# Layer 0 of a four-layer convolution chain: five of nine depthwise taps computed by VectorE and GpSimd, Gelu over pairs of PSUM banks, stores of two steps sent together

## The chip, the cores and the metric

The kernel runs on one core of a Trainium2 chip, all in float32 but for one quantised convolution in a later layer. The time is the device time of that core in microseconds, the median of several runs. A profiled execution gives one more time, its own, and the trace from which all views are taken. In the views PE is TensorE (PEld its weight loads), DVE is VectorE, ACT is ScalarE, POOL is GpSimd and SP is SyncE; SPq is the queue of DMA issues on SP.

## The reference, cut to what matters

The input x has the shape (4, 16, 512, 512): four images, 16 channels. Four layers follow one another. The change concerns layer 0 only, a block with window attention:

```python
pos = depthwise_conv3x3(x, pos_w)          # one 3x3 filter for each channel, padding 1
x = x + pos + pos_b
win = windows_8x8(x * alpha1 + beta1)      # 64 tokens in a window, 16 channels
q, k, v = win @ qkv_w.T + qkv_b            # 2 heads of 8 channels, q scaled by 8 ** -0.5
out = softmax(q @ k.T) @ v
x = x + (out @ proj_w.T + proj_b)
h = gelu((x * alpha2 + beta2) @ fc1_w.T + fc1_b)    # 16 -> 64
x = x + h @ fc2_w.T + fc2_b                # 64 -> 16
```

Layers 1 to 3 are a quantised 3x3 convolution with a batch norm over the whole tensor, a residual pair of 3x3 convolutions, and a 3x3 convolution with a small MLP. Layer 1 needs the largest absolute value of all that layer 0 gives, so it begins after the last store of layer 0.

## The kernel before, in words

`window_attention` works in 64 steps (`STEPS`). A step holds 16 units, by u and vv from 0 to 3. A unit is 32 partitions (two blocks of 16 channels) by 8 rows of 64 columns: 8 windows of 64 tokens, the 512 columns of a matmul. The order of the instructions on every engine is the order in which they are written (`manual_schedule`): nothing is reordered, and an engine whose next instruction waits holds all that is written behind it on that engine. The SP queue, which issues nearly all DMAs, is one of them.

A step n works on three steps' data at once:

- **Attention of step n**, a loop over k = 0 to 7 (half a block column each). `scores` (L353) writes four banks, ScalarE's Exp (L361) takes them in two pairs to e; `values` (L338) turns the values into yt; `attend` (L374) gives two banks, which `divide` transposes on VectorE (L389), takes the reciprocal of the sums (L394) and multiplies on GpSimd (L396); `turn_back` (L403) transposes the result into o, one or more k later. In the loop stand also `turn_keys` (L310: DMAs that bring the next step's y into the order of keys), `send` (L90: up to 5 stores a k) and `highest_output` (L452: one maximum of a finished output).
- **The MLP of step n**: `project` (L409, and L414 on VectorE, which adds to y), then 16 `hidden` units (L421), each with a Gelu on ScalarE (L426) from one bank. `output` (L432, and L437 on VectorE, into xo) of step n stands in step n + 1, after its first scores. xo is one buffer that two steps fill; after an odd step its 32 stores are listed, and `send` issues them later.
- **Queries of step n + 1** (`query`, L319; the copies to g are L324 on ScalarE and L326 on VectorE) and the **depthwise convolution of step n + 2** (L287), both woven into the MLP by a string of letters: d is one tap for one u (four matmuls of 32x32 with 512 columns), q one query, h one hidden unit. When all 9 taps for 4 u are done, `position` adds the bias and writes y (L302 on VectorE for two u, L298 on ScalarE for two). `highest` (L329) takes the maximum of the next y.

The depthwise convolution multiplies the shifted input (x with a border of one) by a 32x32 diagonal matrix of the tap's weights (`taps`, which is `small`, an identity, times `tap0`); nine taps add up in PSUM. A float32 matmul stands in the trace as two records. PSUM has eight banks: 0 to 3 as two pairs, 4 to 7 single. x has two buffers, y three, e three, hid sixteen (one bank each).

After the last step the output of u = 0 to 2 is placed between the last hidden units, with its stores on two queues, SP and GpSimd.

## Time and profile before

| what | value |
|---|---|
| median of 3 runs | 5842.46 us (5837.79 to 5846.63) |
| the profiled execution, its own time | 5832.97 us |
| its span | 5831.2 us |
| TensorE busy | 5512.4 us (95%) |
| VectorE busy | 3723.4 us (64%) |
| ScalarE busy | 3464.1 us (59%) |
| GpSimd busy | 707.4 us (12%) |
| mean granted TensorE clock | 0.987 |
| DMA | 677.47 MB, mean 116 GB/s |

Layer 0 takes the first 21 or so of 40 equal slices of the span. A line of the costliest groups reads: line, engine, operation, output<-input, shape, count | busy us, mean ns of one | idle time of the engine before them, and what ended it. A line of the timeline reads: start, duration, engine, line, operation, count, and in brackets the idle time before it and its releaser. A row of the windows view gives for one stretch its length, the busy time of PE, PEld, DVE, ACT and POOL with counts, the granted clock of TensorE (1.00 is full), the DMA share and GB/s. Matmul records overlap[...], so busy TensorE time is not the sum of their durations.

### The profile page before, as it was taken

The page shows a single profiled execution, that of the slowest core. Times are in us where ns is not written, and L with a number is a line of the kernel's source. Part 1 is how long each engine was busy: PE and PEld are TensorE (multiplying, and loading weights), DVE is VectorE, ACT ScalarE, POOL GpSimd, SP SyncE. Part 2 cuts the span into 40 slices and gives each one's busy share as a digit, 9 for nine tenths or more (in the row PEclk, how much of TensorE's full clock was granted, in tenths as well). Part 3 has the DMA queues.
Part 4 walks back from the last instruction along what each step waited for, and adds up shares of the span by engine and source line. Part 5 has one row for each costly group of instructions (what it writes and reads, how often), then busy time and mean ns, then how long its engine had stood idle before and what let it go on. Part 6 is the DMA issues. An engine that isn't in the chain of part 4 may idle for free. (4 is left out here: it accounts for less than half of the span.)

```text
span 5831.2 us, 268523 instructions
## 1 busy us (share of the span) xinstructions
PE 5512.4 (95%) x120912; PEld 3058.4 (52%) x120912; DVE 3723.4 (64%) x5806; ACT 3464.1 (59%) x4739; POOL 707.4 (12%) x692
## 2 busy tenths in 40 slices
PE   7999999999999999999999676999999999999999
PEld 5666666666666666666666333333333333333333
DVE  4666666666666666666666564666666666666666
ACT  4777777777777777777776453444444444444444
POOL 1111111111111111111111451000000000000000
PEclk9999999999999999999999898999999999999999
DMA  2232323233333333332332796666666666666663
GB/s 78 69 77 68 81 67 72 69 79 70 78 72 75 75 72 77 71 79 69 79 70 47 170 252 169 168 169 171 165 171 167 169 171 166 170 167 170 171 165 103
DMA packets 626194, 677.47 MB, mean 116 GB/s; under 512 B 355856, under 2 KB 485008, under 8 KB 616848
## 3 DMA queue, kind: packets, MB, share of 16 engines
q1 hardware_dynamic: 624240, 658.76, 47.3%
q8 instruction: 953, 15.61, 1.1%
q14 instruction: 201, 1.65, 0.1%
q0 software_dynamic: 512, 1.05, 0.1%
q10 hardware_dynamic: 288, 0.39, 0.0%
HBM read 222.45 MB, written 134.48 MB: 61 GB/s over the span
## 5 line engine op out<-in xcount | busy, mean ns | idle before, releaser
L361 ACT ACTIVATE e<-pair 128x1024 f32<-128x1024 f32 x1024 | 992.9, 1022 | 436.7 <-PE pair L353 436.0
L287 PE MATMUL pair<-x,taps 32*32 32x512 f32 x18432 | 1082.2, 600 | 2.2 <-DVE y L302 1.2
L1205 ACT ACTIVATE hid<-tb,vec 128x512 f32<-128x512 f32 x1024 | 620.0, 688 | 518.1 <-PE tb L1197 518.0
L389 DVE STREAM_TRANSPOSE a<-bank 128x512 f32<-128x512 f32 x1024 | 669.8, 692 | 346.5 <-PE bank L374 313.3
L396 POOL TENSOR_TENSOR t<-a,r 128x512 f32<-128x512 f32 x512 | 542.0, 1059 | 2662.2 <-DVE r L394 2598.5
L426 ACT ACTIVATE hid<-bank,f1b 128x512 f32<-128x512 f32 x1024 | 648.3, 687 | 345.2 <-PE bank L421 281.6
L353 PE MATMUL pair<-g,y 32*128 32x128 f32 x16384 | 762.8, 288 | 29.5 <-ACT y L298 25.8
L353 PEld LDWEIGHTS pair<-g,y 32*128 32x128 f32 x16384 | 650.4, 187 | 189.6 <-issue 77.4
L421 PE MATMUL bank<-y,fc_e 32*32 32x512 f32 x8192 | 738.3, 606 | 1.0 <-DVE y L414 1.0
L1207 DVE TENSOR_SCALAR hid<-tb,vec 128x512 f32<-128x512 f32 x1024 | 695.7, 742 | 2.7 <-PE tb L1197 2.6
L1197 PE MATMUL tb<-ye,mat 32*128 32x512 f32 x4096 | 637.7, 624 | 0.3 <-DVE hid L1207 0.3
L374 PE MATMUL bank<-e,yt 64*32 64x128 f32 x32768 | 610.0, 276 | 28.3 <-DVE yt L346 21.4
L287 PEld LDWEIGHTS pair<-x,taps 32*32 32x32 f32 x18432 | 495.4, 103 | 171.2 <-issue 66.3
L374 PEld LDWEIGHTS bank<-e,yt 64*32 64x32 f32 x32768 | 465.6, 106 | 127.3 <-issue 99.1
L1217 PE MATMUL tb<-hid,mat 128*32 128x512 f32 x4096 | 466.0, 595 | 41.6 <-DVE hid L1207 41.6
L1197 PEld LDWEIGHTS tb<-ye,mat 32*128 32x128 f32 x4096 | 267.0, 183 | 323.4 <-issue 219.9
L1122 PE MATMUL tb<-zo,cw 64*32 64x512 f32 x3096 | 362.8, 594 | 14.8 <-issue 8.9
L338 PE MATMUL bank<-mat,y 128*128 128x128 f32 x2048 | 338.9, 288 | 36.1 <-DVE xo L437 36.0
L1122 PE MATMUL tb<-xo,cw 64*32 64x512 f32 x3096 | 365.0, 599 | 8.4 <-issue 6.6
L1122 PE MATMUL tb<-xe,cw 64*32 64x512 f32 x3072 | 360.3, 599 | 0.0
L1122 PE MATMUL tb<-ho,cw 64*32 64x512 f32 x3072 | 355.2, 591 | 3.1 <-issue 3.1
L1122 PE MATMUL tb<-ze,cw 64*32 64x512 f32 x3072 | 356.8, 594 | 0.0
(180 smaller groups left out, 7051.7 us busy)
## 6 DMA issues: line engine op xcount, KB each, us to landing
x<-in_xw_dram SPq DMA_DIRECT2D x64, 1320.0 KB
zo<-ze SPq DMA_DIRECT2D x512, 128.5 KB
ho<-he SPq DMA_DIRECT2D x512, 128.5 KB
xo<-xe SPq DMA_DIRECT2D x512, 128.5 KB
y<-y SPq DMA_DIRECT2D x2048, 32.0 KB
tx<-x SPq DMA_DIRECT2D x256, 256.0 KB
out_dram<-xe SPq DMA_DIRECT2D x128, 512.0 KB
x<-xo SPq DMA_DIRECT2D x1008, 64.0 KB
```

What stands on the lines that cost most here:

```text
L287: nc.tensor.matmul(bank(u)[quad(vv)], taps[quad(u), tap, :], xts[n][quad(u), vv, dy : dy + WS, dx : dx + BW], start=tap == 0, stop=tap == 8,)
L353: nc.tensor.matmul(bank(u)[:, P * jj : P * jj + P], y2[quad(u), vv, jl + jj].rearrange("p w t -> p (w t)"), g[quad(u), vv, jl + jj].rearra ...
L361: nc.scalar.activation(e[:, 2 * i : 2 * i + 2].rearrange("p u j t -> p u (j t)"), pairs[i], AF.Exp,)
L374: nc.tensor.matmul(bank(4 + 2 * (k % 2) + w)[quad(u), P * jj : P * jj + P], t[half, U * jj + u, w : w + 2].rearrange("p d c -> p (d c)"), ...
L389: nc.vector.transpose(a[:, 512 * w : 512 * w + 512], bank(4 + 2 * (k % 2) + w))
L396: engine.tensor_tensor(t.rearrange("p b w c -> p w b c"), top, r.unsqueeze(3).to_broadcast([P, 2, 16, C]), ALU.mult,)
L421: nc.tensor.matmul(b[quad(k)], fc1[quad(vv), quad(k)], y[quad(vv), u, :], start=True, stop=True,)
L426: nc.scalar.activation(hd, b, AF.Gelu, bias=f1b)
L1122: nc.tensor.matmul(p[r][_quad(2 * f + w)], weights[_half(r), odd, dx, :], src[_half(r), f, dx : dx + W], start=dx == 0, stop=dx == 2,)
L1197: nc.tensor.matmul(p[q], w1[_quad(q), 1 - par, :], inner(src)[_quad(q), f, :], start=True, stop=True,)
L1205: nc.scalar.activation(hd, p[q], AF.Relu, bias=v("l3_b1"))
L1207: nc.vector.tensor_scalar(hd, p[q], v("l3_b1"), 0.0, ALU.add, ALU.max)
```

## The change

Taps 4 to 8 are no longer matmuls. VectorE multiplies tap 8 into a buffer `rest` and adds tap 7 (`begin_rest`: 4 tensor_scalar, 4 scalar_tensor_tensor); GpSimd adds taps 4, 5 and 6 (`add_rest`: twelve times a tensor_scalar into one buffer `rt` and a tensor_tensor that adds it to `rest`). TensorE keeps taps 0 to 3 and adds `rest` by a fifth matmul with `small`. Of the twelve pieces for step n + 3 seven are written at the end of step n behind `begin_rest`, and five in the next step's loop over k, each after a `divide`. The two first steps keep nine taps.

All of PSUM becomes four pairs. Gelu takes a pair of banks, 1024 elements, at a time; `divide` transposes a pair at once; all four positions are on VectorE. The woven string of the MLP becomes ten d, eight h, two q, eight h. e has two buffers, hid eight of a pair each. The 32 stores of two steps are sent at k = 1, ahead of that k's `turn_keys`, where there were five at every k. The last step's output is no longer woven in.

```diff
@@ -169,11 +169,13 @@
     wts = ctx.enter_context(tc.tile_pool(name="w0w", bufs=1))
     ps = ctx.enter_context(tc.tile_pool(name="w0p", bufs=1, space=PSUM))
 
-    pairs = [ps.tile([P, 2, 512], F32, name=f"pair{i}") for i in range(2)]
-    singles = [ps.tile([P, 512], F32, name=f"bank{i}") for i in range(4)]
+    pairs = [ps.tile([P, 2, 512], F32, name=f"pair{i}") for i in range(4)]
 
     def bank(i):
-        return pairs[i // 2][:, i % 2, :] if i < 4 else singles[i - 4]
+        return pairs[i // 2][:, i % 2, :]
+
+    def base(k):
+        return 4 + 2 * ((k + 1) % 2)
 
     def quad(i):
         return slice(32 * i, 32 * i + 32)
@@ -270,6 +272,7 @@
     g = pa.tile([P, V, NJ, NH, T], F32, name="g")
     o = pa.tile([P, V, NJ, NH, T], F32, name="o")
     most = pa.tile([P, STEPS], F32, name="most")
+    rest = pa.tile([P, V, WS, BW], F32, name="rest")
     yts = [pa.tile([P, 4 * U, 3, C], F32, name=f"yt{i}") for i in range(3)]
     for t in yts:
         nc.gpsimd.memset(t, 1.0)
@@ -280,28 +283,48 @@
     def by_row(ap):
         return ap.rearrange("p (a j x) -> p a j x", a=WS, x=WS)
 
-    def depthwise(n, tap, u):
-
+    def shifted(n, tap, rows, vv):
         dy, dx = divmod(tap, 3)
+        return xts[n][rows, vv, dy : dy + WS, dx : dx + BW]
+
+    def depthwise(n, tap, u, n_taps=5):
+
         for vv in range(V):
+            if tap < 4 or n_taps == 9:
+                w, src = taps[quad(u), tap, :], shifted(n, tap, quad(u), vv)
+            else:
+                w, src = small[quad(u)], rest[quad(u), vv]
             nc.tensor.matmul(
-                bank(u)[quad(vv)], taps[quad(u), tap, :],
-                xts[n][quad(u), vv, dy : dy + WS, dx : dx + BW],
-                start=tap == 0, stop=tap == 8,
-            )
+                bank(u)[quad(vv)], w, src, start=tap == 0, stop=tap == n_taps - 1
+            )
+
+    def begin_rest(n):
+        every = slice(0, P)
+        for vv in range(V):
+            nc.vector.tensor_scalar(
+                rest[:, vv], shifted(n, 8, every, vv), tap0[:, 8:9], None, ALU.mult
+            )
+        for vv in range(V):
+            nc.vector.scalar_tensor_tensor(
+                rest[:, vv], shifted(n, 7, every, vv), tap0[:, 7:8], rest[:, vv],
+                ALU.mult, ALU.add,
+            )
+
+    def add_rest(n, i):
+        at, vv = divmod(i, V)
+        t = px.tile([P, WS, BW], F32, tag="rt", name=f"rt{n}_{i}", bufs=1)
+        nc.gpsimd.tensor_scalar(
+            t, shifted(n, 4 + at, slice(0, P), vv), tap0[:, 4 + at : 5 + at], None, ALU.mult
+        )
+        nc.gpsimd.tensor_tensor(rest[:, vv], rest[:, vv], t, ALU.add)
 
     def position(n):
 
         y = px.tile([P, U, N], F32, tag="y", name=f"y{n}", bufs=3)
         for u in range(U):
-            if u // 2:
-                nc.scalar.activation(
-                    by_window(y[:, u]), by_row(bank(u)), AF.Identity, bias=v("pos_b")
-                )
-            else:
-                nc.vector.tensor_scalar(
-                    by_window(y[:, u]), by_row(bank(u)), v("pos_b"), None, ALU.add
-                )
+            nc.vector.tensor_scalar(
+                by_window(y[:, u]), by_row(bank(u)), v("pos_b"), None, ALU.add
+            )
         return y
 
     def turn_keys(y, vv):
@@ -333,7 +356,7 @@
     def values(k):
 
         vv, jl = k // 2, 4 * (k % 2)
-        b, t = bank(4 + 2 * (k % 2)), yts[k % 3]
+        b, t = bank(base(k)), yts[k % 3]
         for jj in range(4):
             nc.tensor.transpose(
                 b[:, P * jj : P * jj + P],
@@ -356,7 +379,7 @@
                     g[quad(u), vv, jl + jj].rearrange("p h t -> p (h t)"),
                     start=True, stop=True,
                 )
-        e = px.tile([P, U, 4, P], F32, tag="e", name=f"e{n}_{k}", bufs=3)
+        e = px.tile([P, U, 4, P], F32, tag="e", name=f"e{n}_{k}", bufs=2)
         for i in range(2):
             nc.scalar.activation(
                 e[:, 2 * i : 2 * i + 2].rearrange("p u j t -> p u (j t)"),
@@ -372,7 +395,7 @@
                 for w in range(2):
                     half = slice(64 * w, 64 * w + 64)
                     nc.tensor.matmul(
-                        bank(4 + 2 * (k % 2) + w)[quad(u), P * jj : P * jj + P],
+                        bank(base(k) + w)[quad(u), P * jj : P * jj + P],
                         t[half, U * jj + u, w : w + 2].rearrange("p d c -> p (d c)"),
                         e[half, u, jj, :],
                         start=True, stop=True,
@@ -385,8 +408,9 @@
     def divide(k, n, engine):
 
         a = px.tile([P, 1024 + 2 * C], F32, tag="a", name=f"a{n}_{k}")
-        for w in range(2):
-            nc.vector.transpose(a[:, 512 * w : 512 * w + 512], bank(4 + 2 * (k % 2) + w))
+        nc.vector.transpose(
+            a[:, 0:1024], pairs[base(k) // 2].rearrange("p w n -> p (w n)")
+        )
         top = a.rearrange("p (w n) -> p w n", w=2)[:, :, 0:512]
         top = top.rearrange("p w (b c) -> p w b c", c=32)[:, :, :, 0:C]
         low = a[:, C : 1024 - C].rearrange("p (w n) -> p w n", w=2)[:, :, 0 : 512 - C : 32]
@@ -407,24 +431,29 @@
             for u in range(U):
                 for vv in range(V):
                     nc.tensor.matmul(
-                        bank(4 + (u + 2) % 4)[quad(vv)], wo[h][quad(u)], o[quad(u), vv, :, h, :],
+                        bank(4 + u)[quad(vv)], wo[h][quad(u)], o[quad(u), vv, :, h, :],
                         start=h == 0, stop=h == 1,
                     )
         for u in range(U):
             nc.vector.scalar_tensor_tensor(
-                y[:, u], bank(4 + (u + 2) % 4), pb, y[:, u], ALU.add, ALU.add
-            )
-
-    def hidden(y, u, vv, b, n):
+                y[:, u], bank(4 + u), pb, y[:, u], ALU.add, ALU.add
+            )
+
+    def hidden(y, u, vv, b):
 
         for k in range(4):
             nc.tensor.matmul(
                 b[quad(k)], fc1[quad(vv), quad(k)], y[quad(vv), u, :],
                 start=True, stop=True,
             )
-        hd = px.tile([P, N], F32, tag="hid", name=f"hid{n}_{u}_{vv}", bufs=16)
-        nc.scalar.activation(hd, b, AF.Gelu, bias=f1b)
-        return vv, hd
+
+    def gelu(pair, name):
+        hd = px.tile([P, 2, N], F32, tag="hid", name=name, bufs=8)
+        nc.scalar.activation(
+            hd.rearrange("p w n -> p (w n)"), pair.rearrange("p w n -> p (w n)"),
+            AF.Gelu, bias=f1b,
+        )
+        return hd
 
     def output(y, xo, hids, us, banks, n):
 
@@ -495,7 +524,7 @@
     for n in range(2):
         for tap in range(9):
             for u in range(U):
-                depthwise(n, tap, u)
+                depthwise(n, tap, u, 9)
         xts[n + 2] = load(n + 2)
         ys[n] = position(n)
     highest(0)
@@ -504,6 +533,9 @@
     for h in range(NH):
         for vv in range(V):
             query(ys[0], h, vv, bank(vv))
+    begin_rest(2)
+    for i in range(7):
+        add_rest(2, i)
     last, xo = None, None
     nc.scalar.preload_act_table_set("natural_log_exp_and_others")
     for n in range(STEPS):
@@ -518,7 +550,7 @@
             elif what == "d" and ahead:
                 depthwise(n + 2, taken[at], at)
                 taken[at] += 1
-                if taken == [9] * U:
+                if taken == [5] * U:
                     ys[n + 2] = position(n + 2)
 
         values(0)
@@ -533,16 +565,19 @@
             ts[k - 1] = divide(k - 1, n, nc.gpsimd)
             if 1 < k < 7:
                 turn_back(ts[k - 2], k - 2)
+            if k == 1:
+                send(8 * U)
             if k % 2 and more:
                 turn_keys(ys[n + 1], k // 2)
+            if k < 6 and ahead:
+                add_rest(n + 2, k + 6)
             highest_output()
-            send(5)
         nc.scalar.preload_act_table_set("gelu_and_others")
         attend(es[7], 7)
         ts[7] = divide(7, n, nc.gpsimd)
         for k in (5, 6, 7):
             turn_back(ts[k], k)
-        free = iter((4, 5, 6, 7, 4, 5))
+        free = iter((6, 7, 4, 5, 6, 7))
         for i, what in enumerate("qqddddqqqqdddddd"):
             block(what, i, bank(next(free)) if what == "q" else None, True)
         if more:
@@ -557,24 +592,29 @@
 
 
 
-        hids, units = [], itertools.cycle((6, 7, 4, 5))
-        for i, what in enumerate("ddddhdhddhqhddhqhddhdhddhdhddhdhddhdhddddhdh"):
+        hids, units = [], iter((2, 3, 2, 0, 3, 2, 3, 2))
+        for i, what in enumerate(10 * "d" + 8 * "h" + "qq" + 8 * "h"):
             if what == "h":
-                q = len(hids)
-                hids.append(hidden(y, q // 4, i % 4, bank(next(units)), n))
-                if not more and q in (5, 9, 13):
-                    u = q // 4 - 1
-                    output(y, xo, hids[q - 5 : q - 1], (u,), (u,), n)
-                    send(8, queues)
+                u, at = len(hids) // 4, i % 4
+                if at % 2 == 0:
+                    pair = pairs[next(units)]
+                hidden(y, u, at, pair[:, at % 2])
+                if at % 2:
+                    hd = gelu(pair, f"hid{n}_{u}_{at}")
+                    hids += [(at - 1, hd[:, 0]), (at, hd[:, 1])]
             else:
-                block(what, i, bank(next(units)) if what == "q" else None)
+                block(what, i, bank(i % 4) if what == "q" else None)
+        if n + 3 < STEPS:
+            begin_rest(n + 3)
+            for i in range(7):
+                add_rest(n + 3, i)
         if n + 4 < STEPS:
             xts[n + 4] = load(n + 4)
         if more:
             nc.scalar.preload_act_table_set("natural_log_exp_and_others")
-        last = (y, xo, hids, range(U), (5, 4, 6, 7), n)
-    output(y, xo, hids[12:], (3,), (3,), n)
-    send(8, queues)
+        last = (y, xo, hids, range(U), (7, 5, 6, 4), n)
+    output(*last)
+    send(8 * U, queues)
     highest_output(2 * U)
     return nc.values_load(flag[0:1, 0:1], min_val=0, max_val=1)
```

## The prediction, made before the change was run

> **What bounds the kernel now.** I first read the page's busy times by engine, then its costliest groups, then engine times by stretch for one step of layer 0 (64 steps, about 3,115 of the 5,831 us), then the timelines of ScalarE, VectorE and GpSimd in it. The maximum over y (L329) runs once a step; from 54.25 to 3171.18 us it starts 63 times more, so a step lasts 3116.9 / 63 = 49.5 us. Let t0 be the end of a step's last turn-back (L403); one t0 is 1395.4, the next 1444.6.
>
> ```profile
> L287 PE MATMUL pair<-x,taps 32*32 32x512 f32 x18432 | 1082.2, 600 | 2.2 <-DVE y L302 1.2
> L396 POOL TENSOR_TENSOR t<-a,r 128x512 f32<-128x512 f32 x512 | 542.0, 1059 | 2662.2 <-DVE r L394 2598.5
> L426 ACT ACTIVATE hid<-bank,f1b 128x512 f32<-128x512 f32 x1024 | 648.3, 687 | 345.2 <-PE bank L421 281.6
> ```
>
> The largest TensorE group is the depthwise (18432 records, 288 a step), and GpSimd has one operation of 1059 ns for each of eight k, with 2662 us idle. The step has three stretches:
>
> ```profile
> core 0: us, PE busy (x) PEld busy (x) DVE busy (x) ACT busy (x) POOL busy (x), PEclk, DMA share, GB/s
> 1395.40:1412.90 17.50, 17.06 (x472) 10.97 (x454) 9.06 (x12) 12.06 (x21) 0.00 (x0) 1.00 0.39 71
> 1412.90:1421.30 8.40, 7.15 (x151) 3.84 (x145) 2.49 (x5) 5.72 (x6) 0.00 (x0) 1.00 0.64 194
> 1421.30:1444.60 23.30, 23.20 (x787) 18.83 (x796) 18.45 (x34) 17.78 (x23) 8.47 (x8) 1.00 0.24 47
> ```
>
> The row from 1395.4 is the MLP: project, hidden layer and Gelu, with most of the depthwise between them. The next leads into the attention loop (first scores, output, first attend); the third is the loop from the first divide to t0. GpSimd works in the third only. Inside the MLP:
>
> ```profile
> 1395.39 2.24 DVE L329 TENSOR_REDUCE most<-y 128x1 f32<-128x2048 f32 x1
> 1398.14 2.72 DVE L414 SCALAR_TENSOR_TENSOR y<-bank,pb,y 128x512 f32<-128x512 f32 x4
> ...
> 1409.73 1.41 DVE L302 TENSOR_SCALAR y<-pair,vec 128x512 f32<-128x512 f32 x2 [5.66 <-PE pair L287]
> ```
> ```profile
> 1400.07 2.75 ACT L426 ACTIVATE hid<-bank,f1b 128x512 f32<-128x512 f32 x4 [3.86 <-PE bank L421]
> 1406.10 3.57 ACT L426 ACTIVATE hid<-bank,f1b 128x512 f32<-128x512 f32 x6 [0.28 <-PE bank L421]
> ```
>
> From 1400.07 to 1412.85 ScalarE pauses 1.5 us only: sixteen Gelus and two positions pace this part, and TensorE, full of depthwise, just keeps up; VectorE idles 5.66 us for the depthwise. In the loop one k takes about 2.9 us, near VectorE's sum: 1.31 (two transposes) + 0.35 + 0.65, and 0.64 where a peak is taken. So TensorE's 95% is not a bound that gives back all that it is relieved of.
>
> [...] the quantiser's row below agrees, 1118 ns for 1024 elements with a per-partition scalar. [...] L1143 agrees on the speed (1024 in 695 ns)[...]. [...] the clock halves[...]. This trace has it in the first step without a depthwise:
>
> ```profile
> L1010 POOL TENSOR_SCALAR xe<-xe,inv_x 128x1024 f32<-128x1024 f32 x42 | 47.0, 1118 | 36.3 <-DMA xe<-x 32.5 <-ACT qe L1013 3.7
> ```
> ```profile
> 3174.00:3176.00 2.00, 1.42 (x19) 0.30 (x16) 2.00 (x5) 0.14 (x1) 0.00 (x0) 1.00 0.18 34
> 3176.00:3178.00 2.00, 2.00 (x31) 0.62 (x32) 0.65 (x1) 1.88 (x3) 0.00 (x0) 0.74 0.28 53
> 3178.00:3180.00 2.00, 2.00 (x30) 0.56 (x26) 0.75 (x1) 0.69 (x1) 0.00 (x0) 0.50 0.73 126
> ```
>
> The sixth column falls from 1.00 to 0.50 and stays there to 3194; that step's first divide comes at 3199.28, t0 (3171.2) + 28.1.
>
> **The change, part by part** (times from t0 on).
>
> *TensorE.* Depthwise falls from 288 to 160 records a step. At the trace's rate (33 records in a 1.69 us piece, one lasting 0.6: 0.034 each) that frees 128 x 0.034 = 4.4 us. Project is done at about 3.2 now; the ten tap-units put behind it (80 records, 2.7 us, the first of them beside project) end near 5.2, and only then the first hidden matmul is issued (3.5 now).
>
> *ScalarE.* Sixteen Gelus at 0.687 become eight of 1024 elements; the Exp of that shape takes 1.02: 11.0 becomes 8.2 us. The two positions (1.26) leave. Eight Gelus from about 6.2 end at 14.6; the table load (1.28) ends at 15.9 where it now ends at 18.8.
>
> *VectorE.* After L414 (ends 5.3) four positions of 0.746 end at 8.3. Two queries follow eight hidden units; their g copies (0.75 each) end near 10.9. Then `begin_rest`: four tensor_scalars at 0.43 (0.695 for 1024[...]) and four scalar_tensor_tensors at 0.75 (L1223): the first `rest` quarter is ready at 10.9 + 1.7 + 0.75 = 13.4, the last at 15.6. The next values copy (L346) is queued behind them and comes 1 us late, which delays one bank of the output. The pair transpose saves about 0.1 us per k.
>
> *The lead-in.* First scores' Exp ends near 18, output's copies near 19.5, scores, values and attend of k=1 follow as now: first divide at about 21.3, where it is 25.9 and 24.4 in two neighbouring steps. With the loop unchanged (23.3) the step would be 44.6, about 44 with the pair transposes.
>
> *GpSimd.* Twelve pieces a step, each a tensor_scalar (0.103 for the smallest memset, plus half of 1118 - 103: 0.61) and a tensor_tensor (1.06). The second waits for the first, and the next piece for it. The trace has no such wait within GpSimd; a start behind VectorE comes 0.15 after the producer (1384.56 to 1384.71). [...] I take 0.12, twice: 1.91 a piece. The chain starts at 13.4. Seven pieces end at 26.8, and **the first divide's multiply is queued behind them** though its data are there at about 23; turn-back of k=0 then holds VectorE, and TensorE behind its banks. In the loop a multiply (1.11) and a piece (1.91) alternate: 3.0 us per k, no less than VectorE's. To t0: 13.4 + 12 x 1.91 + 6 x 1.11 for k=0 to 5 + 3.1 for the last two and their turn-back = **46.1**. That beats 44.6, so GpSimd sets the end: 49.5 - 46.1 = 3.4 us a step.
>
> *SP and stores.* An issue takes about 0.68. Thirty-two stores go at k=1 of each even step: 21.8 us, with the eight issues of the first turned keys behind them, then the other 24. The first keys land near 48, while the next step's values need them near 60; the next x load issues some 18 us into the step after, over 35 us ahead of its `begin_rest`: nothing. The stores' DMA work is the same. They now finish before xo is written again; that wait was 103 us in 19 cases over the layer (the tile view of xo), mostly beside TensorE's own output. It is inside the 49.5, and I credit nothing more. Two buffers of e instead of three cost nothing: the attend that frees one precedes it on TensorE.
>
> *Once.* Start: eight VectorE operations before the first values copy, 5 us. End: output is no longer mixed with the last hidden layer; 16 matmuls, four copies and 32 stores on two queues (16 x 0.65) come after it, where layer 1 waits: 10 us.
>
> **Sum.** The full cycle runs in 61 steps: 61 x 3.4 = 207, less 15: 192. Profiled execution 5833.0 - 192 = 5641; the median lies 9.5 above that execution: about **5650**.
>
> **Rivals.**
> *All of it hidden:* no waits within GpSimd give 13.4 + 12 x 1.67 + 6 x 1.06 + 3.1 = 42.9, and VectorE's loop sets 44: 61 x 5.5 - 15 = 320 gained, 5522. Against it: the alternation leaves no slack.
> *The halved clock:* [...] 28.1 for the lead-in, less 2.8 for paired Gelus, plus 22.7: 48.0, 1.5 gained: 5833 - 92 + 15 + 9.5 = 5766; if it only delays the output by 3: 47.0, 5705. For it: the rows above. Against: ten tap-units fill TensorE up to the hidden layer, and GpSimd's queue hides a late first divide.
> *Slower: GpSimd becomes a bound that is longer than the step was.* 23.2 + 12 pieces passes 49.5 at 2.19 us a piece, only 0.28 above mine. A strided tensor_scalar priced as two-input work gives 1.06 + 1.06 + 0.24 = 2.36 and 51.5: 5833 + 122 + 15 + 9.5 = 5980. [...] For it: the thin margin, and every k's turn-back depends on this queue. Against: the L1010 row, and multiplies that hold 1059 beside VectorE's transposes.
> *No change:* what TensorE loses was hidden, and the Gelus wait for the same thing: 5842.
>
> **How the numbers follow.** A measurement of this kernel tells 0.2% (12 us) from no change. GpSimd chain as forecast, 0.48 (its own range 5560 to 5760: pieces of 1.80 to 2.05, and a few steps at half clock); all hidden, 0.10; halved clock in most steps, 0.12, a third of it at or above no change; GpSimd longer than the old step, 0.28; no effect, 0.02. Faster 0.66, same 0.05, slower 0.29. The range runs from 5510 to 5950, leaving out a part of the slower case.
>
> **What would show it.** Right: L287 with 62 x 160 + 2 x 288 = 10496 records; Gelu 512 times near 1.02 us; GpSimd busy over 25 us a step, its multiply late against L394, and L403 waiting for GpSimd; steps of 46 us; TensorE's clock at 1.00. Wrong: GpSimd's tensor_scalar above 0.8 us or pieces above 2.19; a clock of 0.5 in the hidden layer of most steps; L403 waiting for nothing with steps of 44 us.

## The result, and the profile after

| | before | changed |
|---|---|---|
| median | 5840.12 us (4 runs) | 6881.2 us (4 runs, 6874.53 to 6895.52) |
| ratio | | 1.1798, 95% interval 1.1753 to 1.1842 |
| span of the profiled execution | 5831.2 us | 6872.7 us |
| mean step of layer 0 | 49.5 us | 66.1 us |
| mean granted TensorE clock | 0.987 | 0.90 |

The change makes the kernel 18% slower; the forecast was 5650 us and faster. The step is read as in the prediction, from the maximum over y (L352 in the changed kernel): its first and last start, at 55.7 and 4221.1 us, lie 63 steps apart. That is 4165.4 us against the 3116.9 us of before, 1048.5 us more: the whole loss of 1041 us lies in the steps.

The costliest groups on the page of the changed kernel (busy us, mean ns of one | idle time before it and its releaser):

```profile
L319 POOL TENSOR_TENSOR rest<-rest,rt 128x512 f32<-128x512 f32 x744 | 967.4, 1300 | 1385.8 <-DVE rest L308 1328.8
...
L316 POOL TENSOR_SCALAR rt<-x,tap 128x512 f32<-128x512 f32 x744 | 1183.1, 1590 | 67.0 <-DMA x<-in_xw_dram 30.4
...
L452 ACT ACTIVATE hid<-pair,f1b 128x1024 f32<-128x1024 f32 x512 | 550.8, 1111 | 596.0 <-PE pair L445 594.3
L342 PE MATMUL pair<-y,wg 32*32 32x512 f32 x4096 | 619.7, 774 | 248.3 <-ACT g L347 185.8
```

GpSimd's tensor_scalar takes 1590 ns where the prediction had 610, its tensor_tensor 1300 where it had 1060. GpSimd also idles 1329 us for VectorE to begin the sum: it starts late as well as being slow. And a line of another kind stands here: TensorE, in its query matmuls, idles 186 us for a copy of g on ScalarE.

The three stretches of one step (t0 = 1437.42), in the columns of the prediction's table:

```profile
core 0: us, PE busy (x) PEld busy (x) DVE busy (x) ACT busy (x) POOL busy (x), PEclk, DMA share, GB/s
1437.42:1462.97 25.55, 21.41 (x380) 7.83 (x364) 13.60 (x19) 11.33 (x13) 2.27 (x2) 0.77 0.23 68
1462.97:1472.94 9.97, 8.98 (x168) 5.41 (x169) 4.96 (x7) 5.64 (x6) 9.33 (x8) 0.89 0.01 2
1472.94:1505.65 32.71, 25.17 (x720) 18.35 (x720) 18.49 (x26) 16.79 (x20) 31.11 (x25) 0.85 0.19 35
```

The MLP grew from 17.5 to 25.6 us, the lead-in from 8.4 to 10.0, the loop from 23.3 to 32.7. GpSimd is busy 31.1 of the loop's 32.7 us, and the clock is below 1.00 in all three. The MLP's start in the timeline of ScalarE, then of VectorE (in brackets the idle time and what ended it):

```profile
1434.21 0.69 ACT L347 ACTIVATE g<-pair,gb 128x512 f32<-128x512 f32 x1 [3.34 <-PE pair L342]
1436.95 0.69 ACT L347 ACTIVATE g<-pair,gb 128x512 f32<-128x512 f32 x1 [2.05 <-PE pair L342]
1438.97 0.69 ACT L347 ACTIVATE g<-pair,gb 128x512 f32<-128x512 f32 x1 [1.33 <-PE pair L342]
1441.71 1.26 ACT L347 ACTIVATE g<-pair,gb 128x512 f32<-128x512 f32 x2 [2.05 <-PE pair L342]
1445.02 0.69 ACT L347 ACTIVATE g<-pair,gb 128x512 f32<-128x512 f32 x1 [2.05 <-PE pair L342]
```
```profile
1449.73 2.73 DVE L438 SCALAR_TENSOR_TENSOR y<-pair,pb,y 128x512 f32<-128x512 f32 x4 [9.55 <-issue]
...
1460.57 4.18 DVE L308 SCALAR_TENSOR_TENSOR rest<-x,tap,rest 128x512 f32<-128x512 f32 x4
```

Six query copies stretch over 11.5 us, nearly each after a wait of 2 us for its own matmuls. `project` is queued behind the queries on TensorE, so L438, which updates y, begins 12.3 us after t0 (L414, the same operation, 2.7 before), and `begin_rest` stands behind it on VectorE. Later in the same step, GpSimd:

```profile
1461.49 1.62 POOL L319 TENSOR_TENSOR rest<-rest,rt 128x512 f32<-128x512 f32 x1 [23.28 <-DVE rest L308]
1463.20 1.88 POOL L316 TENSOR_SCALAR rt<-x,tap 128x512 f32<-128x512 f32 x1
1465.17 1.27 POOL L319 TENSOR_TENSOR rest<-rest,rt 128x512 f32<-128x512 f32 x1
...
1480.27 1.26 POOL L319 TENSOR_TENSOR rest<-rest,rt 128x512 f32<-128x512 f32 x1
1481.49 1.05 POOL L420 TENSOR_TENSOR t<-a,r 128x512 f32<-128x512 f32 x1
1482.52 1.56 POOL L316 TENSOR_SCALAR rt<-x,tap 128x512 f32<-128x512 f32 x1
```

Seven pieces run until 1481.5. The first divide's reciprocal was ready at 1474.6, so its multiply (L420) waits 6.9 us in GpSimd's queue, and VectorE behind it, as the waits view has it for 1000 to 2000 us (us in total, times, longest):

```profile
DVE o L427 <- POOL t L420: 134.2, 75, 4.9
...
PEld pair L342 <- ACT g L347: 100.6, 45, 3.1
```

The weight loads of the queries thus wait 100.6 us there for ScalarE's copies. In the kernel before, over the same 1000 us:

```profile
PEld bank L319 <- ACT g L324: 2.5, 8, 0.8
```

### The profile page after: what moved, and what is told of

Same layout as the page of the kernel before. It is cut to its first block, busy times and chain, and to the rows that moved or that the text cites. A ratio compares the mean times of both kernels' runs of the same rounds, so it can differ in the third digit from the quotient of the medians.

```text
span 6872.7 us, 252582 instructions
## 1 busy us (share of the span) xinstructions
PE 5894.8 (86%) x112976; PEld 2882.3 (42%) x112976; DVE 4144.1 (60%) x5918; ACT 3323.0 (48%) x4098; POOL 2830.4 (41%) x2180
## 5 line engine op out<-in xcount | busy, mean ns | idle before, releaser
L319 POOL TENSOR_TENSOR rest<-rest,rt 128x512 f32<-128x512 f32 x744 | 967.4, 1300 | 1385.8 <-DVE rest L308 1328.8
L316 POOL TENSOR_SCALAR rt<-x,tap 128x512 f32<-128x512 f32 x744 | 1183.1, 1590 | 67.0 <-DMA x<-in_xw_dram 30.4
L452 ACT ACTIVATE hid<-pair,f1b 128x1024 f32<-128x1024 f32 x512 | 550.8, 1111 | 596.0 <-PE pair L445 594.3
L342 PE MATMUL pair<-y,wg 32*32 32x512 f32 x4096 | 619.7, 774 | 248.3 <-ACT g L347 185.8
L411 DVE STREAM_TRANSPOSE a<-pair 128x1024 f32<-128x1024 f32 x512 | 633.2, 1237 | 268.3 <-PE pair L397 165.9
L397 PE MATMUL pair<-e,yt 64*32 64x128 f32 x32768 | 630.6, 286 | 105.4 <-DVE yt L369 105.3
L361 PE MATMUL pair<-mat,y 128*128 128x128 f32 x2048 | 381.9, 315 | 360.6 <-DVE a L411 293.2
L297 PE MATMUL pair<-x,taps 32*32 32x512 f32 x8512 | 597.7, 776 | 1.4 <-DVE y L325 1.4
L420 POOL TENSOR_TENSOR t<-a,r 128x512 f32<-128x512 f32 x512 | 538.7, 1057 | 143.0 <-DVE r L418 136.4
L445 PE MATMUL pair<-y,fc_e 32*32 32x512 f32 x8192 | 552.4, 700 | 46.1 <-ACT hid L452 44.2
L397 PEld LDWEIGHTS pair<-e,yt 64*32 64x32 f32 x32768 | 484.3, 110 | 203.3 <-issue 196.8
L438 DVE SCALAR_TENSOR_TENSOR y<-pair,pb,y 128x512 f32<-128x512 f32 x256 | 174.5, 744 | 490.9 <-issue 486.9
```

The costliest lines, as they stand in the source:

```text
L316: nc.gpsimd.tensor_scalar(t, shifted(n, 4 + at, slice(0, P), vv), tap0[:, 4 + at : 5 + at], None, ALU.mult)
L319: nc.gpsimd.tensor_tensor(rest[:, vv], rest[:, vv], t, ALU.add)
L342: nc.tensor.matmul(b[quad(u)], wg[h][quad(vv)], y[quad(vv), u, :], start=True, stop=True)
L397: nc.tensor.matmul(bank(base(k) + w)[quad(u), P * jj : P * jj + P], t[half, U * jj + u, w : w + 2].rearrange("p d c -> p (d c)"), e[half, ...
L411: nc.vector.transpose(a[:, 0:1024], pairs[base(k) // 2].rearrange("p w n -> p (w n)"))
```

## The experiments

Each ratio is to the kernel before, measured beside it. "First transpose" below is the start of the first `divide` (L411 in the changed kernel), counted from t0; means are over the whole steps between 1500 and 2100 us of each trace.

**What a GpSimd operation costs (e1_forms).** The kernel before, with eight forms, four instructions each, ahead of the loop over steps: tensor_scalar with one operation on 1024 contiguous elements, and on 512 contiguous (L514), shifted and strided (to L522); tensor_tensor on 512 contiguous (L524) and strided.

```diff
+    for _ in range(4):      # L514; the others change the view or the operation
+        nc.gpsimd.tensor_scalar(f512, ys[0][:, 0], w, None, ALU.mult)
```

> The kernel before, with eight forms of GpSimd operation, four of each, written to a scratch tile ahead of the first step: tensor_scalar of 1024 contiguous elements, of 512 contiguous from y, of 512 contiguous from x at an even and at an odd start, of 8 x 64 rows out of x (row step 66) at an even and at an odd start; tensor_tensor of two contiguous operands of 512, and of two out of x at an odd start. The prediction's price: 1.12 us for 1024, 0.61 for every tensor_scalar of 512, 1.06 for both tensor_tensors. If the rows of the shifted view are what costs, only the 8 x 64 forms stand near 1.56. If the start of the view is (an odd element), the odd forms stand above the even ones. If 512 elements with a scalar from memory cost 1.56 in any form, all stand there. If the fan-out of the multiplier in divide made 1.06 cheap, the plain tensor_tensor stands near 1.27.

The timeline of GpSimd (each line is four instructions with the gaps between them):

```profile
42.07 11.67 POOL L512 TENSOR_SCALAR forms<-y,tap 128x1024 f32<-128x1024 f32 x4 [24.99 <-issue]
53.83 6.53 POOL L514 TENSOR_SCALAR forms<-y,tap 128x512 f32<-128x512 f32 x4
...
80.33 6.53 POOL L522 TENSOR_SCALAR forms<-x,tap 128x512 f32<-128x512 f32 x4
86.94 5.28 POOL L524 TENSOR_TENSOR forms<-y 128x512 f32<-128x512 f32 x4
```

Contiguous and strided cost the same, 1.63 us with the gap, so the shifted view is innocent. But 1024 elements take 2.9 us where the row that the prediction drew on (L1010) has 1.118. That row is `tensor_scalar(t, t, ix, ROUND, ALU.mult, ALU.add)`: two operations. The changed kernel's form has one, with None for the second. The tensor_tensor, an addition, costs 1.3, not the 1.06 of `divide`, a multiplication whose second operand is a broadcast of 32 values; which of the two differences makes the price was not tested.

**Without GpSimd's pieces, with the queries in pairs, and both (e2 to e4).** e2 leaves out taps 4 to 6 (the first diff), and so does e4. e3 and e4 issue two queries, to both banks of a pair, before either is copied (the second):

```diff
     def add_rest(n, i):
+        return
```

```diff
-                query(ys[n + 1], asked[at], at, b, scalar)     # matmuls, then the copy
+                held.append(query(ys[n + 1], asked[at], at, b, scalar))   # matmuls only
                 asked[at] += 1
+                if len(held) == 2:
+                    held.pop(0)()      # the two copies
+                    held.pop(0)()
```

> The changed kernel without the twelve GpSimd pieces; taps 4, 5 and 6 are left out of the sum. Theory P (the pieces are dearer than predicted, 3.02 us, and hold the first divide's multiply): the first divide stays at t0 + 35.5, the loop goes back to about 22.7, steps of 58 us, 62 x 7.1 = 440 us less than the change, about 6440. Theory Q (queries wait for the copies of their pair's other bank, at a halved clock) alone: the loss lies ahead of the loop, so nearly nothing is won, above 6750.

> The changed kernel, but two queries are issued to the two banks of a pair before the copies of both. Theory Q: the 12 us of queries with a copy between each two shrink to 4 or less, the first rest is ready near t0 + 14 instead of 24, steps of about 57 us, near 6400. Theory P alone: the pieces fill the step, 12 x 3.02 + 8 x 1.06 = 45 us, and an earlier start of them is worth what it moves: also some gain, but the clock stays low; above 6700 if the query waits are not what delayed the MLP.

> Both: queries by pairs and no GpSimd pieces (taps 4, 5 and 6 left out). If P and Q are all of it, the step is the prediction's other chain: lead-in near 21 to 25, loop 22.7, 44 to 48 us, 5530 to 5780. If something else took part (the halved clock in the hidden layer, one bank order, the burst of stores), it stays above 5900.

Measured: e2 6399.26 (1.0951, 1.087 to 1.1032), e3 6411.81 (1.0973, 1.0924 to 1.1022), e4 5877.07 (1.0066, 1.0044 to 1.0088). With the queries in pairs the end of L438 moves from 13.3 us after t0 to 5.6 (e3). So both causes are real, and either alone leaves about half of the loss. Even without any piece, e4 isn't faster than before: there is a third cause.

**The two-operation form (e5, e6).** The same product, with a zero added; e6 has the queries in pairs too.

```diff
-            t, shifted(n, 4 + at, slice(0, P), vv), tap0[:, 4 + at : 5 + at], None, ALU.mult
+            t, shifted(n, 4 + at, slice(0, P), vv), tap0[:, 4 + at : 5 + at], 0.0,
+            ALU.mult, ALU.add,
```

> The changed kernel with GpSimd's tensor_scalar given a second operation (times the tap, plus 0.0), the form of the quantiser's row that the prediction took its price from; the sums are the same. If the price belongs to that form, the operation takes 0.6 instead of 1.56 us, a piece 2.05 instead of 3.02, and 12 x 0.96 = 11.5 us of GpSimd go; but with the queries unmended the other chain (58 to 61 us a step without any pieces) sets the end, so the time is that of the kernel without pieces, about 6400. If the form does not matter (the view, the float scalar), it stays at 6880.

> Both mends: two-operation tensor_scalar and queries by pairs; it computes all. Theory P with the price in the form: GpSimd's chain is 13.5 + 12 x 2.05 + 8 x 1.1 and some, 47 to 48 us, beside the 50.4 us of the kernel without pieces: about 5880 to 5950. If a third cause stands outside both (the halved clock, pairs in the loop), that one keeps it above 5840; if the pieces still hold the multiplies, near 6000 or above.

The group on the page of e6, then ScalarE's query copies in its timeline:

```profile
L316 POOL TENSOR_SCALAR rt<-x,tap 128x512 f32<-128x512 f32 x744 | 521.3, 701 | 66.4 <-DMA x<-in_xw_dram 29.8
```
```profile
1389.00 1.27 ACT L351 ACTIVATE g<-pair,gb 128x512 f32<-128x512 f32 x2 [1.44 <-PE pair L343]
1390.49 2.42 ACT L351 ACTIVATE g<-pair,gb 128x512 f32<-128x512 f32 x4 [0.23 <-PE pair L343]
```

Adding an operation makes the instruction faster: 1590 to 701 ns. The six copies now take 3.9 us in place of 11.5. Measured: e5 6439.66 (1.104, 1.0992 to 1.1089), e6 5952.15 (1.0207, 1.0175 to 1.024). The two repairs add up: 0.076 for the form alone, 0.083 for the queries alone, 0.159 together. Of the loss, 0.021 is left.

**The stores alone, and the nine taps put back (e7, e8).** e7 is the kernel before with `send(8 * U)` at k = 1 in place of `send(5)` at every k. e8 has the changed layout of PSUM and paired queries, but nine taps on TensorE, woven among the hidden units.

```diff
+            if k == 1:
+                send(8 * U)
             if k % 2 and more:
                 turn_keys(ys[n + 1], k // 2)
             highest_output()
-            send(5)
```
```diff
-        for i, what in enumerate(10 * "d" + 8 * "h" + "qq" + 8 * "h"):
+        for what in "dddd hh dd hh dd qq dd hh ddd hh ddd hh ddd hh dddd hh ddd hh".replace(" ", ""):
...
-                if taken == [5] * U:
+                if taken == [9] * U:
```

> The kernel before with one edit of the change: 32 stores sent at k = 1 instead of five at every k. The prediction: nothing or a gain, since the wait of xo for its stores (103 us in 19 cases) goes: 5740 to 5840. Rival: the first turned keys, behind 32 issues of 0.68, come late for the next step, or the burst collides with the load of x: above 5860.

> The changed kernel with all nine taps back on TensorE, woven among the hidden units, and queries by pairs; four pairs in PSUM, Gelu by pairs and stores in one go stay. If the kernel without pieces lost its last microseconds to a halved clock in the thin hidden layer, TensorE is full again, the clock stays at 1.00, and the lead-in comes back to 22 to 24: 47 to 48 us a step, about 5740 to 5800. If it lost them to pairs as units of waiting in the loop (3.17 us a k instead of 2.9), the loop stays at 24 us, and with a lead-in of 25, near 5830 to 5900.

e7: 5776.51 (0.9903, 0.9873 to 0.9933). The output's wait for earlier stores, 103.2 us in 19 cases before, is absent from its trace; the stores in one go are a small gain. e8: 6058.66 (1.0388, 1.0355 to 1.0421), with the clock at 1.00 in its steps. On the paired layout nine taps on TensorE are thus slower than four and a sum (e6), though the order of the strings differs too. Against e7, which has nine taps and the same stores on the layout of before, e8 loses 0.0485 with the clock at 1.00 in both: this layout, with its order, costs something that isn't the clock.

**Single banks, and work to hold the clock (e9, e10).** e9 has five taps on VectorE and GpSimd in the two-operation form on the layout of before. e10 is e6 with eight matmuls of 256 columns, whose result nobody reads, ahead of each of the last four Gelus.

```diff
-    pairs = [ps.tile([P, 2, 512], F32, name=f"pair{i}") for i in range(4)]
+    pairs = [ps.tile([P, 2, 512], F32, name=f"pair{i}") for i in range(2)]
+    singles = [ps.tile([P, 512], F32, name=f"bank{i}") for i in range(4)]
```
```diff
+                    if len(hids) >= 8 and more:
+                        for r in ((2, 3) if at == 1 else (0, 1)):
+                            for k in range(4):
+                                nc.tensor.matmul(
+                                    bank(r)[quad(k)][:, 0:256], fc1[quad(r), quad(k)],
+                                    y[quad(r), u, 0:256], start=True, stop=True,
+                                )
                     hd = gelu(pair, f"hid{n}_{u}_{at}")
```

> The change's five taps on VectorE and GpSimd (GpSimd's multiplication in its two-operation form) and the stores of two steps in one go, on the layout of before: banks 4 to 7 are tiles of their own, a Gelu follows each hidden unit, each bank is transposed by itself, queries are copied one by one. Against the run with the two-operation form and the queries by pairs (5952) it takes away only the pair tiles. Theory (what is left of the loss is the pair as the unit of waiting): the loop goes from 24 back to 22.5 to 23 per step and the first divide comes 2 to 4 earlier, so a step of 47.5 to 49 and 5690 to 5780, at or under the stores alone (5776). Rival (the halved clock in the lead-in, where the TensorE has no taps to weave, costs it): the first divide stays at 26 to 27 after the last turn-back, the clock of 0.5 stays in the records, 5880 to 5960. Second rival (16 single Gelus cost more than 8 pairs now that they are bunched): slower than 5952.

> The run with the two-operation form and the queries by pairs (5952), with 8 matrix multiplications of 256 columns added ahead of each of the last four Gelus of a step, whose results are written to a bank that is not read from. Theory of the pairs: the clock may rise in that stretch, but it waits for the Gelus anyway; 5940 to 5990. Rival (the halved clock): the clock of 0.5 goes from the records, the output comes 1 to 2 earlier in each step, 5840 to 5900. If the added work lies on the path at the low clock: 6000 to 6080.

e9: 5942.76 (1.0193, 1.0166 to 1.022), no better than e6: the theory of the pairs is refuted for this arrangement. e10: 5905.79 (1.0139, 1.0115 to 1.0162), a little better. Where e6's clock falls to 0.50 in most steps, e10's stays at 1.00 in most, so the rival holds in part.

**The same kernel with and without the fall.** The traces hold a comparison of their own, since the clock doesn't fall in every step. Of 58 steps (the first two and the last few are left out) it stays at full from t0 to the first transpose in 24 of e4, 22 of e6, 31 of e9 and 47 of e10, and falls to 0.50 for a stretch in all the others. Two neighbouring steps of e4 and two of e9, from t0 to t0 (columns: length, PE busy with count, clock, DMA share, GB/s):

```profile
1761.85:1814.24 52.39, 48.14 (x1271) 0.93 0.35 78
1814.24:1862.67 48.43, 43.89 (x1255) 1.00 0.28 67
```
```profile
1547.59:1596.89 49.30, 46.56 (x1246) 1.00 0.27 64
1596.89:1648.72 51.83, 51.02 (x1278) 0.90 0.35 77
```

The steps that keep the clock take 48.9 us on average in e4 (51.3 where it falls), 50.3 in e6 (51.7) and 50.0 in e9 (52.5). The fall goes with 1.4 to 2.5 us of a step, and e4's steps without it are a little shorter than the mean step of before (49.5), so the third cause is mostly this. Comparing steps is no experiment, since what makes the clock fall might lengthen a step by itself; e10 is the experiment. Its steps that keep the clock take 50.3 us as in e6, there are only more of them, and that accounts for most of its gain. At full clock e9 and e6 are 0.3 us apart: single banks bring next to nothing in that order of the strings.

**The woven order, the early sum (e11, e12).** In e11 the ten tap strings stand among the hidden units. The sum is the first tap of each unit, so `begin_rest` may stand ahead of the hidden layer:

```diff
-            if tap < 4 or n_taps == 9:                       # depthwise: taps 0 to 3, then the sum
+            if tap > 0 or n_taps == 9:                       # the sum, then taps 0 to 3
...
-        for what in "dddddddddd hhhhhhhh qq hhhhhhhh".replace(" ", ""):
+        begin_rest(n + 3)                 # and seven pieces of add_rest
+        for what in "dd hh dd hh dd hh dd hh d qq hh d hh hh hh".replace(" ", ""):
...
-        begin_rest(n + 3)                 # and seven pieces, behind the hidden layer
```

e12 exchanges the banks' roles on top of that:

```diff
-                bank(u)[quad(vv)], w, src, ...       # depthwise in pairs 0 and 1
+                bank(4 + u)[quad(vv)], w, src, ...   # in single banks; hidden units, queries, Gelu in the pairs
```

> As the kernel on single banks, with the sum of the five taps as the first of each unit's TensorE taps in place of the last, so that the next sum starts on VectorE ahead of the hidden layer, and with the ten later tap strings woven among the hidden units. Theory of the pairs, with the lead-in as what is left: Gelus start about 8 earlier (ten strings of 0.8 no longer ahead of the first hidden unit), 5600 to 5690. Rival (GpSimd's chain sets the end: 12 pieces of 2.15 and seven divides of 1.06): no gain over the kernel on single banks, within 30 of it.

> As the woven kernel, with the roles of the banks exchanged: the depthwise taps and the output in the four single banks, the hidden units, the queries and the Gelus in the two pairs (Gelu over pairs, queries copied two by two). It keeps all four parts of the change. Theory (a pair costs only where two readers or writers share it at different times): 20 to 60 under the woven kernel by 8 Gelus of 1.11 in place of 16 of 0.69, 5560 to 5650. Rival (two pairs are too few, each hidden pair waits for the Gelu two ahead): 0 to 100 over the woven kernel.

e11: **5678.21 (0.9751, 0.9728 to 0.9774)**, faster than before and than the stores alone. e12: 5991.6 (1.0275, 1.025 to 1.0301), over 300 us slower than e11 and beyond what its rival gave. Its clock falls in 47 of the 58 steps, around the end of the Gelus (18.1 us after t0). But its 11 other steps take 50.0 us, 3 more than e11's, so the clock isn't all of it, and the rest was not separated. TensorE's clock in neighbouring 2-us rows of one step, from 10 us after t0, in e9 and then in e11 (columns: length, PE busy with count, clock, DMA share, GB/s):

```profile
1606.89:1608.89 2.00, 2.00 (x36) 0.59 0.07 24
1608.89:1610.89 2.00, 2.00 (x36) 0.50 0.00 0
1610.89:1612.89 2.00, 2.00 (x36) 0.50 0.00 0
1612.89:1614.89 2.00, 2.00 (x18) 0.50 0.00 0
```
```profile
1575.87:1577.87 2.00, 2.00 (x51) 1.00 0.04 8
1577.87:1579.87 2.00, 2.00 (x25) 1.00 0.63 174
1579.87:1581.87 2.00, 2.00 (x44) 1.00 1.00 422
1581.87:1583.87 2.00, 2.00 (x24) 1.00 0.20 83
```

TensorE is called busy for 2.00 of 2.00 us in both; only the clock tells the rows apart. It isn't the whole difference between the kernels: e11 keeps the clock in all 58 steps and takes 46.9 us a step, e9 51.1, and those of e9's steps that keep the clock too take 50.0. About 1.1 of the 4.2 us go with the clock, and 3.1 with the order and the early sum themselves.

**Which part of e11 did it (e13 to e15).** e13 is e11 with the ten strings bunched again, e15 is e9 with the woven order alone. e14 puts the pairs and the Gelu over pairs back on e11: the changed kernel with four repairs.

```diff
-        for what in "dd hh dd hh dd hh dd hh d qq hh d hh hh hh".replace(" ", ""):    # e13, against e11
+        for what in "dddddddddd hhhhhhhh qq hhhhhhhh".replace(" ", ""):
```
```diff
-                hids.append(hidden(y, q // 4, next(vvs), bank(next(units)), n))       # e14, against e11
+                hidden(y, u, at, pair[:, at % 2])
+                if at % 2:
+                    hd = gelu(pair, f"hid{n}_{u}_{at}")
+                    hids += [(at - 1, hd[:, 0]), (at, hd[:, 1])]
```
```diff
-        for what in "dddddddddd hhhhhhhh qq hhhhhhhh".replace(" ", ""):               # e15, against e9
+        for what in "dd hh dd hh dd hh dd hh d qq hh d hh hh hh".replace(" ", ""):
```

> The woven kernel (ratio 0.975), with its ten later tap strings back in one bunch ahead of the hidden units; the sum is still the first tap and starts early. Theory of the clock (TensorE's work thins out in the bunched order and the clock falls to 0.50 from 10 after the last turn-back): 0.50 is back in the hidden layer, first transpose after the last turn-back at 25 to 27 in place of 22.6, ratio 1.00 to 1.02. Rival (the early start of the sum is what gained): ratio 0.97 to 0.985.

> The changed kernel with its pairs of banks and its Gelu over pairs kept, and four repairs: the two-operation form on GpSimd, the queries copied two by two, the sum as first tap with the early start, the tap strings woven among the hidden units. Theory (pairs are neutral once the queries are issued two by two and the clock holds): within 40 of the woven kernel on single banks, ratio 0.97 to 0.985, clock 1.00. Rival (a pair as the unit of waiting costs 2 to 4 per step, as the woven kernel with exchanged banks and the one with nine taps on TensorE would say): ratio 1.00 to 1.03.

> The kernel on single banks (ratio 1.019), with only the order of the strings changed: ten tap strings woven among the hidden units. The sum is still the last tap and starts behind the hidden layer. Theory of the clock: it stays at 1.00, the first transpose after the last turn-back comes at 22.5 to 24, ratio 0.975 to 0.99. Rival (the late sum holds GpSimd's divides or the second string's last taps back): ratio 1.00 to 1.02 with the clock at 1.00.

| | sum late | sum early |
|---|---|---|
| strings bunched | e9 1.0193 | e13 1.0363 (1.0339 to 1.0387) |
| strings woven | e15 1.0428 (1.0406 to 1.0451) | e11 0.9751 |

Neither half works alone, against what I expected of e15. In e13 the clock falls in every step, in half of them from 10 us after t0 on, and is 0.50 from 16 to 22; the first transpose comes at 28.6 (22.6 in e11). How much of that is the clock can't be read off, since no step keeps it. In e15 the clock holds through the hidden layer and falls behind it in 36 of 58 steps, which are no longer than the 22 others (53.4 and 54.0 us): its loss isn't the clock. The late sum is in the way twice. On VectorE it stands ahead of the values copy, for which output's weight loads and matmuls wait (the waits view from 1000 to 2000 us has 58.8 and 42.4 us for that, and no such line in e11). On GpSimd, in one step's timeline, the multiply comes late and VectorE waits for it:

```profile
1585.29 1.28 POOL L318 TENSOR_TENSOR rest<-rest,rt 128x512 f32<-128x512 f32 x1
1586.53 1.06 POOL L418 TENSOR_TENSOR t<-a,r 128x512 f32<-128x512 f32 x1
```
```profile
1581.92 0.36 DVE L416 RECIPROCAL r<-a 128x32 f32<-128x32 f32 x1
...
1587.62 0.71 DVE L425 STREAM_TRANSPOSE o<-t 128x512 f32<-128x512 f32 x1 [2.07 <-POOL t L418]
```

The reciprocal is ready at 1582.3; the multiply starts 4.2 us later, behind the seven pieces. e14: 5835.31 (0.9999, 0.9984 to 1.0014), with the clock at 1.00. The pairs with all that goes with them (Gelus and transposes over pairs, queries copied two by two, the last output no longer woven in) cost 0.025 against e11, nearly all of it in the steps (49.4 and 46.9 us). Its Gelus take as long from first to last (5.7 to 16.7 us after t0; 4.5 to 15.5 in e11) though eight of 1.11 are 2.1 us less work than sixteen of 0.69, and the first transpose comes at 24.7 in place of 22.6. Which of e14's waits for pairs makes the 2 us wasn't separated.

## Why the prediction was wrong, point by point

The sum foretold 46.1; the step shown above has 68.2 (t0 1437.42 to 1505.65). Term by term of the GpSimd chain, which did set the end:

| term | predicted | measured in that step |
|---|---|---|
| start, first quarter of `rest` ready | 13.4 | 24.07 |
| seven pieces | 13.4 | 20.00 |
| five pieces and multiplies in the loop | 5 x 3.02 = 15.1 | 5 x 3.91 = 19.56 |
| the last multiplies and the turn-back | 4.2 | 4.60 |
| sum | 46.1 | 68.23 |

(This step is one of the longer ones; the mean is 66.1. The seven pieces are measured without the first tensor_scalar, which GpSimd had done at 1438.2, before `rest` was there.)

So the path was right, GpSimd's chain as what sets the end, and two of its terms were mis-sized: the start by 10.7 us and the twelve pieces by 11.1.

- **"Each a tensor_scalar (... half of 1118 - 103: 0.61)" failed.** The row taken had another form of the instruction. One operation costs 1.56 (the changed kernel), two cost 0.70 (e6). What I left open in the piece was only the waits (an estimate of 0.12 each; the gap measured 0.09), not the operation itself. The slower rival had the right mechanism and point: pieces passed its 2.19 and came to 3.02, but its reason, a strided view priced as two-input work, was wrong (e1).
- **What more elements cost** depends on the form too: with two operations the second 512 elements cost 0.42 us (1.118 for 1024 less 0.701 for 512), with one 1.29 (2.92 less 1.63, e1).
- **"A tensor_tensor (1.06)" was mis-sized**: 1.27 undisturbed, an addition of two full operands.
- **"Project is done at about 3.2 now" failed.** The prediction left the queries ahead of `project` where they were. Of the start's +10.7, 9.7 come from there: L438 ends 15.0 us after t0, not 5.3. A query to one bank waited for the copy out of the other bank of the pair, and TensorE's clock was 0.50 there (from 1436 to 1448 us): the page's L342 averages 774 ns (L319 before: 599 from 1000 to 2000 us). The wait came with the tile, which now spans both banks: two queries issued together removed it (e3), and with banks 4 to 7 as tiles of their own, queries one by one, the six copies of a step take 3.77 us (e11). The profile of before already had pairs in use for its first queries, and I didn't look at how those waited: from 60.7 us on TensorE stands 1.50 us before every second query, for VectorE's copy of g.
- **The halved clock** was a rival at 0.12 and is part of the answer. "Ten tap-units fill TensorE up to the hidden layer" was true and not enough: the clock falls in the hidden layer, behind them (0.59 and then 0.50 in e9's rows above). That filling TensorE would hold it was my estimate; the runs show only that with added matmuls it fell in fewer steps (11 of 58 in e10, 36 in e6). What decides when it falls was not shown.
- **"First divide at about 21.3" failed**: with no pieces at all (e4) it is 25.6 (25.2 before). The Gelus do end earlier (15.9, against 17.4 before), but from there to the first transpose takes 9.7 us in place of 7.8. In the 34 steps of e4 whose clock falls there the first transpose comes at 26.7, in the 24 others at 24.2. So about 1.4 of the 4.3 us missing go with the clock; the other 2.9 stand at full clock, and which wait makes them is open.
- **"Multiplies that hold 1059 beside VectorE's transposes"** was true of those two operations (1057 in the changed kernel), but in the sum the engines do slow each other. Four L308 take 4.18 us beside GpSimd's pieces in the changed kernel, 2.73 without them (e4). By what means was not shown.
- **Right**: the count of depthwise matmuls (8512 and 1984 for the sum: 10496), GpSimd's chain as what sets the end, the first multiply queued behind the pieces, VectorE's turn-back held by it. VectorE's tensor_scalar took 0.48 (0.43 foretold, an estimate), a paired Gelu 1.11 (1.02), a pair's transpose 1.24 against 1.31 for two banks (0.1 less was my estimate). The stores cost nothing; I credited no gain, and they bring 0.0097 (e7).

## What to carry to other kernels

Price an operation from a row with the same number of operations and the same kinds of operands, or leave the range open on that side; a row with the same name is not enough. When work moves off an engine, ask what still fills that engine around each thin stretch, and whether the moved work lies ahead of something urgent on its new queues: here the move paid (0.9751, against 0.9903 for the stores alone) only when the sum was started early and TensorE's remaining work was spread out, both together, and on single banks; with the pairs (e14) it came out even. Before blaming the clock, compare the steps that keep it with those that lose it in the same trace. Merging two banks into one tile merged their waits here (the queries' weight loads waited 100.6 us in 1000 for ScalarE's copies, 2.5 before): follow every writer of the new tile to the reader that now holds it.

## What the runs showed of the hardware that was not expected

- GpSimd's tensor_scalar on 128x512 float32: 1.56 us with one operation, 0.70 with a second that adds zero; on 1024 elements 2.9 with one, 1.12 with two.
- GpSimd's tensor_tensor: 1.27 us for an addition of two full operands, 1.06 for a multiplication with one of them a broadcast of 32 values.
- Where GpSimd's first addition runs beside VectorE's four scalar_tensor_tensors, one of the two pays, never both: either VectorE's four take 4.18 us in place of 2.73 and the addition 1.62 (all 62 steps of the changed kernel and of e9), or VectorE keeps its 2.73 and the addition takes 2.95 (61 of 62 steps of e11 and of e15; e3 has 33 of the first kind and 29 of the second).
- A TensorE that the profile calls busy all the time may run at half clock: 36 matmul records in 2 us at 0.50 (e9), 24 to 51 in the same stretch at 1.00 (e11). The number of records in a row doesn't predict it, and the same program keeps the clock in some steps and loses it in others (24 and 34 in e4). What decides between them, and why e13's clock stays low longer than e9's, is open.
